# One norm scheme for both attention layers of a four-layer network, the last strip's convolution taps on GpSimd, and a new order of squares, means and index loads

## The chip, the cores and the metric

The kernel runs on one core of one Trainium2 chip. The metric is the device time of one execution in microseconds, the median of several runs. A core has five instruction queues that matter here: TensorE (PE), VectorE (DVE), ScalarE (ACT), GpSimd (POOL) and SyncE (SP). SP issues nearly all DMAs. Each queue runs its instructions in order.

## The reference

A batch of four images of 256 channels on 64 x 64 places goes through four layers, each `x = x + layer(gn(x))`. The change touches the two attention layers only:

```python
# gn: 32 groups of 8 channels; as written here a group's mean and variance are taken
# over axes 1, 2 and 4 of the view (B, H, W, G, C/G) of an array that holds (B, C, H, W)
x = x + _L0_conv_ref(_gn(x), ...)   # attention layer
x = x + _L1_conv_ref(_gn(x), ...)   # attention layer
x = x + _L2_conv_ref(_gn(x), ...)   # mamba layer
x = x + _L3_conv_ref(_gn(x), ...)   # grouped mamba layer

# an attention layer
y = mhsa(x, ...)                     # gated scan down the image (tanh, sigmoid, 1x1 convolutions)
qkv = to_windows(y) @ qkv_w.T + qkv_b            # 64 windows of 64 places
logit = einsum('bpc,bqc->bpq', q_win * SCALE, k_win)   # window means
_, idx = top_k(logit, 4)             # each window attends to the places of 4 windows
out = softmax(q k_g.T * SCALE) v_g   # 8 heads of 32
out = out + depthwise_conv3x3(v, lepe_w) + lepe_b
return out @ wo_w.T + wo_b
```

Since gn reads the array as (B, H, W, C), its groups are pairs of columns of the image: one mean and one variance for two columns over all channels and rows.

## The kernel before, in words

The four images are worked through one after the other, with x of one image held in SBUF (128 partitions x 2 x 4096). `attention_layers` runs two layers; each has a scan phase, `routing` and a window phase. An image is cut into eight strips of eight columns.

**Scan phase.** For each strip it takes the normalised x (`lay["xn"][s]`), makes two hidden layers and the gated scan into `y`, and one strip later the keys and values, which go to a DRAM buffer `kvd`, window by window. The values also go into `vimg`, over whose rows the 3 x 3 depthwise convolution is taken. The norm of the strips is laid in between by `gn_four`, two strips ahead; strips 0 and 1 must be there when the phase begins.

**Routing.** Window means give a 64 x 64 table of logits, and `idx` holds the places of the four best windows.

**Window phase** (`window_phase`, the object of the change). Its loop runs over 32 pairs of windows, i = 0 to 31, with `sj, a = divmod(i, 4)`: four pairs belong to strip sj. The order of all work is written out by hand. For pair i:

- `gather(i + 3)` issues eight DMAs of 128 KB from `kvd` into `kv` (eight buffers, so four pairs). `indices(i + 4)` loads the places into registers of SP before. For pairs 0 and 1 half of the gathers go through ACT's queue.
- `scores` (TensorE, L546) writes into two PSUM buffers, h = 0 and 1. `smallest` (DVE, L558) reduces them to the least value, since the scores are held with the opposite sign. `exps` (ACT, L569) takes exponentials and sums. `normalise` takes the reciprocal (DVE, L581) and scales eight slices on POOL (L584). `turn` (TensorE, L597) transposes, `turned` evicts half on DVE (L608) and half on ACT (L610). `values` (TensorE, L623) multiplies with the values, and `own_rows` (DVE, L634) adds the result to `vimg`.
- In pairs a = 1 and 2, `project` (TensorE, L233) multiplies the strip before with `wo` and its `add` (DVE, L644) adds the result to x. In four pairs a query of strip 6 or 7 is made. `double` moves queries to the other half of the partitions.

Beside this main work each pair carries extra steps from lists:

- `taps`: steps of the convolution of the last two strips on POOL, one a pair. A tap there is a weigh (L254, tile `tap`, tag "sq", one buffer) and an add (L257); the first one of a half is L269. There are 17 steps for each half m of the channels. `dve_taps` are nine single instructions on DVE (L271) for m = 0 of strip 7, popped in pairs with a = 0 or 3.
- `mids` and `ends`: steps of the norm. If a second attention layer follows (`nxt`), strips 0 and 1 of x are normalised by `gn`: sums (DVE, L143), a matmul for the mean (L134), the difference on POOL (L151), its square on ACT (L156, tag "sq"), a reduction on DVE (L160), a matmul, and the scaling on POOL (L168 a power of -0.5, L172). Otherwise `stats` takes only the statistics of strips 0 to 6, for the mamba layer: sums (L200), matmul (L195), mean (L206), four squares of x with the mean as bias, each with its sum (ACT, L215), matmul, variance (L221).
- Results of these small matmuls, projections and queries share one PSUM buffer, tag "mm".

At the start of the phase SP runs `indices(0)`, gathers 0 to 2 with their indices from `idx`, then `load_row`: two DMAs (L493, L494) that bring all places through DRAM into one row of a partition, from which pairs 4 and on are loaded. In the first layer `load_scan_weights(nxt)` (L115, 1 MB) follows.

Of the kernel before, what the change touches and what calls it, by code (L numbers as in the profile page):

```python
# [44 lines left out]
class Net:  # L45
# [33 lines left out]
    def attention_layers(self, x, w_drams, v_drams):  # L79
        tc, nc = self.tc, self.nc  # L80
        with ExitStack() as ctx:
# [107 lines left out]
            def stats(s, psum):  # L189
# [20 lines left out]
                def square(g):  # L210
                    if g == 0:
                        box["s2"] = self.small.tile([P, 4], F32, tag="gn_s2", name="gn_s2")
                        box["sq"] = norm.tile([P, 2, 8, S], F32, tag="xn", name="gn_sq")
                    two = slice(2 * g, 2 * g + 2)
# [5 lines left out]
                def variance():  # L220
                    nc.vector.tensor_copy(self.gvar[:, 4 * s : 4 * s + 4], box["pv"][:, 0:4])  # L221

                return (
                    sums, lambda: columns("pm", box["s1"]), mean,
                    *(lambda g=g: square(g) for g in range(4)),
                    lambda: columns("pv", box["s2"]), variance,
# [250 lines left out]
            def window_phase(lay, work, psum, idx, nxt, taps):  # L477
# [21 lines left out]
                def indices(i):  # L499
                    if 3 < i < n_pair:  # L500
# [150 lines left out]
                indices(0)  # L651
                for i in range(3):
                    gather(i)
                    indices(i + 1)
                load_row()
# [5 lines left out]
                taps = taps + lepe(lay, NW - 1, pool=True)[17:]  # L661
                dve_taps = lepe(lay, NW - 1)[:9]

                mids, ends, left = {}, {}, []
# [8 lines left out]
                if nxt:  # L673
                    load_scan_weights(nxt)
                    for s in range(2):
                        i = 7 + 4 * s
                        plan(gn(nxt, s, lambda: psum), (ends, i), (ends, i + 1), (mids, i + 2),
                             (ends, i + 3), (mids, i + 4), (ends, i + 4), (mids, i + 5))
                else:

                    for s in range(NW - 1):
                        i = 4 * s + 7
                        plan(stats(s, lambda: psum), (ends, i), (ends, i + 1), (mids, i + 2),
                             (ends, i + 2), (mids, i + 3), (ends, i + 3), (mids, i + 4),
                             (ends, i + 4), (mids, i + 5))
                for i in range(n_pair):
# [3 lines left out]
                    if i:  # L690
# [3 lines left out]
                        turn(i - 1, 1)  # L694
                        smallest(i, 1)
# [6 lines left out]
                    normalise(i, 0)  # L702
                    if a == 3 and sj + 2 in (NW - 2, NW - 1):
# [17 lines left out]
                    for t in taps[i : i + 1]:  # L721
                        t()
                    if a in (0, 3) and i and dve_taps:
                        dve_taps.pop(0)()
# [9 lines left out]
                    indices(i + 4)  # L734
# [1437 lines left out]
```

## Time and profile before

| | us |
|---|---|
| median of 3 runs | 11914.07 (11912.61 to 11917.38) |
| profiled execution | 11903.13 |
| its span | 11901.3 |
| first-layer window phases, first to last L584 | 254.8, 251.6, 248.0, 251.2 |
| second-layer window phases, first to last L584 | 224.5, 223.4, 231.3, 233.5 |

The span is the time from the first to the last instruction of the profiled execution. A row of the busy times by stage gives start and end in us, the length, then for each engine its busy time and the number of instructions, then the granted TensorE clock (1.00 is full speed), the share of the DMA engines and GB/s. In a timeline row stand start, duration, engine, line, operation, output and inputs, shapes, and in brackets how long the engine had been idle and what ended that. PEld is the loading of weights into TensorE. A queue letter behind an engine's name (SPq) marks what its sequencer does, such as issuing a DMA.

### The profile page before, as it was taken

How to read it: one execution, taken by the hardware profiler on the slowest of the kernel's cores; microseconds unless marked ns; L12 is line 12 of the kernel's file. 1: busy time of each engine (PE TensorE's matmuls, PEld its weight loads, DVE VectorE, ACT ScalarE, POOL GpSimd, SP SyncE). 2: the span in 40 equal slices, each digit the busy share in tenths (PEclk: the TensorE clock that was granted, in tenths of full speed). 3: DMA queues.
4: the chain of work that ended last, by engine and by line, in shares of the span. 5: the costliest groups of instructions: out<-in, count | busy, mean ns of one | idle time of the engine just before them, and what ended most of it. 6: DMA issues, size and time to landing. Idle time of an engine off the chain costs nothing. (4 is left out here: it accounts for less than half of the span.)

```text
span 11901.3 us, 192225 instructions
## 1 busy us (share of the span) xinstructions
PE 10069.9 (85%) x71104; PEld 5762.7 (48%) x71104; DVE 9868.8 (83%) x8422; ACT 7006.9 (59%) x13096; POOL 8695.6 (73%) x5918
## 2 busy tenths in 40 slices
PE   8998887777899888777789988877778998887777
PEld 4564454444456455444445645544444564554444
DVE  6677998998767799899866779989987677998998
ACT  4565554776456555577645655557764565555776
POOL 4566886898456688689845668868984566886897
PEclk9998998999999899899999989989999998998998
DMA  3344454554334455455433445545543344554554
GB/s 96 101 133 137 173 178 144 171 181 159 89 99 137 138 172 175 147 169 181 157 88 101 133 139 172 176 147 169 181 158 92 98 134 139 173 175 145 169 175 154
DMA packets 682505, 1742.09 MB, mean 146 GB/s; under 512 B 88896, under 2 KB 194896, under 8 KB 681312
## 3 DMA queue, kind: packets, MB, share of 16 engines
q1 hardware_dynamic: 676448, 1721.41, 44.7%
q8 instruction: 563, 9.22, 0.3%
q10 hardware_dynamic: 5120, 8.39, 0.3%
q14 instruction: 374, 3.06, 0.1%
HBM read 1601.52 MB, written 94.39 MB: 142 GB/s over the span
## 5 line engine op out<-in xcount | busy, mean ns | idle before, releaser
L1016 POOL TENSOR_TENSOR hc<-h,cb 128x1024 f32<-128x1024 f32 x2056 | 4807.7, 2350 | 785.6 <-DVE h L1010 341.4
L1010 DVE TENSOR_TENSOR_SCAN h<-da,m_state,pb 128x1024 f32<-128x1024 f32 x1248 | 2920.2, 2340 | 163.1 <-DVE pb L1004 4.3
L962 PE MATMUL y<-ident,hc 128*128 128x128 f32 x16384 | 2345.2, 290 | 404.4 <-POOL hc L1016 333.7
L962 PEld LDWEIGHTS y<-ident,hc 128*128 128x128 f32 x16384 | 2043.7, 150 | 1127.6 <-POOL hc L1016 575.0
L1004 DVE TENSOR_TENSOR pb<-du,pb 128x1024 f32<-128x1024 f32 x1672 | 2024.4, 1211 | 118.9 <-PE pb L934 116.8
L946 ACT ACTIVATE da<-delta,m_v 128x1024 f32<-128x1024 f32 x1672 | 1899.4, 1141 | 135.7 <-DVE h L1010 118.9
L934 PE MATMUL pb<-m_parts,pick 128*128 128x512 bf16 x3312 | 1081.8, 411 | 835.0 <-DVE h L1010 768.7
L584 POOL TENSOR_SCALAR pr<-pr,sm,zero 128x256 f32<-128x256 f32 x2048 | 1136.1, 569 | 533.6 <-DVE sm L581 530.2
L569 ACT ACTIVATE pr<-sc,mn 128x256 f32<-128x256 f32 x2048 | 952.7, 477 | 552.4 <-DVE sm L581 359.9
L934 PEld LDWEIGHTS <-pick 128*128 128x128 bf16 x3312 | 264.0, 101 | 1779.8 <-DVE h L1010 977.2
L558 DVE TENSOR_REDUCE mn<-sc 128x4 f32<-128x1024 f32 x512 | 629.6, 1231 | 528.3 <-PE sc L546 527.0
L1010 DVE TENSOR_TENSOR_SCAN h<-da,pb 128x1024 f32<-128x1024 f32 x424 | 969.3, 2286 | 55.6 <-ACT m_u L1704 0.5
L920 POOL TENSOR_TENSOR bb<-du,bb 128x1024 f32<-128x1024 f32 x376 | 888.5, 2363 | 118.7 <-DMA bb<-m_cd 108.3
L597 PE MATMUL pt_ps<-ident,pr 128*128 128x128 f32 x4096 | 663.9, 297 | 85.0 <-POOL pr L584 40.2
L1010 DVE TENSOR_TENSOR_SCAN h<-dap,m_state,bb 128x1024 f32<-128x1024 f32 x288 | 672.2, 2334 | 65.9 <-ACT dap L946 46.1
L233 PE MATMUL conv_ps<-att_y,att_wb 128*128 128x512 f32 x1536 | 686.7, 597 | 3.0 <-DVE gvar L221 3.0
L546 PE MATMUL sc<-kv,q_swap 32*64 32x128 f32 x8192 | 599.4, 286 | 11.4 <-DMA kv<-kv_dram 8.8
L946 ACT ACTIVATE dap<-delta,m_v 128x1024 f32<-128x1024 f32 x376 | 419.8, 1116 | 308.5 <-DVE h L1010 245.8
L546 PE MATMUL sc<-kv,att_y 32*64 32x128 f32 x7168 | 580.1, 287 | 17.4 <-DMA kv<-kv_dram 13.7
L597 PEld LDWEIGHTS pt_ps<-ident,pr 128*128 128x128 f32 x4096 | 471.5, 148 | 225.6 <-POOL pr L584 138.4
L271 DVE SCALAR_TENSOR_TENSOR lp<-vimg,att_v,lp 128x512 f32<-128x512 f32 x672 | 507.7, 755 | 30.8 <-DVE lp L271 1.0
L546 PEld LDWEIGHTS sc<-kv,att_y 32*64 32x64 f32 x7168 | 434.0, 139 | 153.3 <-issue 58.8
(300 smaller groups left out, 17799.4 us busy)
## 6 DMA issues: line engine op xcount, KB each, us to landing
cb<-m_cd SPq DMA_DIRECT2D x2048, 512.0 KB, 3.8
kv<-kv_dram SPq DMA_DIRECT2D x1984, 128.0 KB, 2.8
bb<-m_cd SPq DMA_DIRECT2D x376, 512.0 KB, 5.5
kv_dram<-kst SPq DMA_DIRECT2D x128, 256.0 KB, 3.9
kv_dram<-vn SPq DMA_DIRECT2D x128, 256.0 KB, 4.1
q_swap<-att_y SPq DMA_DIRECT2D x96, 256.0 KB, 4.4
m_pe<-in_pe_dram SPq DMA_DIRECT2D x32, 512.0 KB, 4.5
out_dram<-yo SPq DMA_DIRECT2D x64, 256.0 KB, 2.4
```

Source lines behind the costliest of these rows:

```text
L233: nc.tensor.matmul(ps, w[:, k, w0 + m * P : w0 + (m + 1) * P], src[:, k], start=(k == 0), stop=(k == 1),)
L546: nc.tensor.matmul(sc[h][b * 64 : b * 64 + 64, r, w, m, :], (own(sj, m) if r == b else swap[sj % 2][:, m])[rows, 2 * a + w], kv[i, w][rows ...
L569: nc.scalar.activation(t[:, g].rearrange("p j r t -> p r j t"), sc[h][:, :, g // 2, g % 2, :].rearrange("p r (j t) -> p r j t", j=2), AF.E ...
L584: nc.gpsimd.tensor_scalar(t[:, g], t[:, g], s[:, g : g + 1], self.zero, ALU.mult, ALU.add)
L597: nc.tensor.transpose(pt[h][j][:, g, :], t[:, g, j].rearrange("p r t -> p (r t)"), self.ident,)
L920: nc.gpsimd.tensor_tensor(pb[i], slots[i][0]["du"], pb[i], ALU.mult)
L934: nc.tensor.matmul(pb[i][:, ss], self.pick[:, n : n + 1].to_broadcast([P, P]), blk["parts"][:, ss], start=True, stop=True,)
L946: nc.scalar.activation(da[i], blk["delta"], AF.Exp, scale=blk["a"](n))
L962: nc.tensor.matmul(blk["y"][:, ss], t[:, ss], self.ident, is_transpose=True, start=(n == 0 and ss.start % NT == 0), stop=(n == DS - 1 and ...
L1004: nc.vector.tensor_tensor(pb[i], blk["du"], pb[i], ALU.mult)
L1010: nc.vector.tensor_tensor_scan(h[i][:, ss], da[i][:, ss], pb[i][:, ss], state, ALU.mult, ALU.add)
L1016: nc.gpsimd.tensor_tensor(hc[i][:, ss], h[i][:, ss], cb[i][:, ss], ALU.mult)
```

## The change

The diff in full. `gn` for the next layer is replaced by `stats` with two new steps: `deviation` (the power over 4 columns) and `scale` (per two columns, subtract the mean and multiply, from x, on POOL), at the ends of pairs 13, 14 (strip 0) and 17, 18 (strip 1). The tile of the squares becomes the normalised tile. Both layers now use one plan: the mean goes to a new list `begins`, run before `smallest(i, 1)`; the squares lie in pairs a = 1 and 2, two each; the variance or deviation is in `begins` too. All 34 steps of strip 7's taps are on POOL; a second step is popped in pairs a = 1, 2, between the two `normalise`. `load_row` comes ahead of the first gather, and pairs 2 and 3 take their places from the row as well. `load_scan_weights` is called in pair 4.

```diff
@@ stats
-            def stats(s, psum):
+            def stats(s, psum, lay=None):
...
                         box["sq"] = norm.tile([P, 2, 8, S], F32, tag="xn", name="gn_sq")
+                        if lay:
+                            lay["xn"][s] = box["sq"]
...
+                def deviation():
+                    rstd = self.small.tile([P, 8], F32, tag="gn_rstd", name="gn_rstd")
+                    box["rstd"] = rstd = rstd[:, 0:4]
+                    nc.vector.tensor_scalar(rstd, box["pv"][:, 0:4], 1e-5, None, ALU.add)
+                    nc.gpsimd.tensor_tensor(
+                        rstd, rstd, self.minus_half.to_broadcast([P, 4]), ALU.pow
+                    )
+
+                def scale(*gs):
+                    for g in gs:
+                        two = slice(2 * g, 2 * g + 2)
+                        nc.gpsimd.tensor_scalar(
+                            box["sq"][:, :, two], xs[:, :, two], box["mean"][:, g : g + 1],
+                            box["rstd"][:, g : g + 1], ALU.add, ALU.mult,
+                        )
+
                 return (
                     sums, lambda: columns("pm", box["s1"]), mean,
                     *(lambda g=g: square(g) for g in range(4)),
-                    lambda: columns("pv", box["s2"]), variance,
+                    lambda: columns("pv", box["s2"]),
+                    *((deviation, lambda: scale(0, 1), lambda: scale(2, 3)) if lay else (variance,)),
                 )
@@ window_phase
                 def indices(i):
-                    if 3 < i < n_pair:
+                    if 1 < i < n_pair:
...
                 indices(0)
+                load_row()
                 for i in range(3):
                     gather(i)
                     indices(i + 1)
-                load_row()
...
-                taps = taps + lepe(lay, NW - 1, pool=True)[17:]
-                dve_taps = lepe(lay, NW - 1)[:9]
-
-                mids, ends, left = {}, {}, []
+                last_taps = lepe(lay, NW - 1, pool=True)
+                taps = taps + last_taps[17:] + last_taps[:17]
+
+                begins, mids, ends, left = {}, {}, {}, []
...
-                if nxt:
-                    load_scan_weights(nxt)
-                    for s in range(2):
-                        i = 7 + 4 * s
-                        plan(gn(nxt, s, lambda: psum), (ends, i), (ends, i + 1), (mids, i + 2),
-                             (ends, i + 3), (mids, i + 4), (ends, i + 4), (mids, i + 5))
-                else:
-
-                    for s in range(NW - 1):
-                        i = 4 * s + 7
-                        plan(stats(s, lambda: psum), (ends, i), (ends, i + 1), (mids, i + 2),
-                             (ends, i + 2), (mids, i + 3), (ends, i + 3), (mids, i + 4),
-                             (ends, i + 4), (mids, i + 5))
+                for s in range(2 if nxt else NW - 1):
+                    i = 4 * s + 7
+                    plan(stats(s, lambda: psum, nxt), (ends, i), (ends, i + 1), (begins, i + 2),
+                         (mids, i + 2), (ends, i + 2), (mids, i + 3), (ends, i + 3),
+                         (ends, i + 4), (begins, i + 5), (ends, i + 6), (ends, i + 7))
...
                         turn(i - 1, 1)
+                        for t in begins.get(i, ()):
+                            t()
                         smallest(i, 1)
...
                     normalise(i, 0)
+                    if a in (1, 2) and taps:
+                        taps.pop(0)()
...
                         own_rows(i - 1)
-                    for t in taps[i : i + 1]:
-                        t()
-                    if a in (0, 3) and i and dve_taps:
-                        dve_taps.pop(0)()
+                    if taps:
+                        taps.pop(0)()
...
                     indices(i + 4)
+                    if i == 4 and nxt:
+                        load_scan_weights(nxt)
                     for t in ends.get(i, ()):
                         t()
```

## The prediction

> **What bounds the kernel now.** I read the page first, then cut the trace by stage. The page gives no engine as the bound:
>
> ```profile
> span 11901.3 us, 192225 instructions
> PE 10069.9 (85%) x71104; PEld 5762.7 (48%) x71104; DVE 9868.8 (83%) x8422; ACT 7006.9 (59%) x13096; POOL 8695.6 (73%) x5918
> ```
>
> The change lies in the window phases alone, two in each of the four batches. I marked each by the first and the last normalising instruction on POOL (L584): the first layer's four take 254.8, 251.6, 248.0 and 251.2 us, the second layer's 224.5, 223.4, 231.3 and 233.5. Both run the same 32 pairs; they differ in the norm work laid beside them. So I cut them at pairs 7 and 19, and summed the busy times of pairs 7 to 18, where the first layer prepares strips 0 and 1 of its successor. First layer (one row of four, then the sum over the four), then second layer:
>
> ```profile
> 290.77:399.52 108.75, 95.78 (x1754) 71.64 (x1747) 67.59 (x105) 60.15 (x219) 77.90 (x115) 0.80 0.46 134
> sum 437.52, PE 380.20 PEld 285.35 DVE 270.13 ACT 240.69 POOL 311.54; mean PE 95.05 PEld 71.34 DVE 67.53 ACT 60.17 POOL 77.89
> ```
>
> ```profile
> 753.81:838.38 84.57, 80.12 (x1756) 59.27 (x1749) 65.49 (x105) 66.90 (x241) 65.89 (x109) 1.00 0.60 167
> sum 346.82, PE 325.94 PEld 243.97 DVE 261.75 ACT 267.88 POOL 263.52; mean PE 81.48 PEld 60.99 DVE 65.44 ACT 66.97 POOL 65.88
> ```
>
> The reader is to see 437.52 against 346.82 us, no engine full in the slower, and a granted TensorE clock of 0.80 there against 1.00. The timeline of the first layer says why (POOL, ACT, DVE and POOL rows of one pair):
>
> ```profile
> 317.62 1.19 POOL L257 TENSOR_TENSOR vimg<-vimg,tap 128x512 f32<-128x512 f32 x1
> ...
> 318.85 1.06 ACT L156 ACTIVATE gn_sq<-att_xn 128x1024 f32<-128x1024 f32 x1 [4.89 <-POOL vimg L257]
> 319.93 1.22 DVE L160 TENSOR_REDUCE gn_s<-gn_sq 128x4 f32<-128x1024 f32 x1 [1.23 <-ACT gn_sq L156]
> ...
> 322.59 1.63 POOL L584 TENSOR_SCALAR pr<-pr,sm,zero 128x256 f32<-128x256 f32 x3 [3.78 <-DVE sm L581]
> ```
>
> The square sits in ACT's order ahead of the exponentials, and cannot start until the tap's add on POOL has freed the one "sq" buffer that both use. ACT stands 4.89 us, DVE stands behind the square with the reduction, and POOL then waits 3.78 us for the reciprocal queued behind that. All of it is one queue waiting for another.
>
> **The change, part by part.** "Per phase" is one window phase; there are four of each layer.
>
> *Norm of the next layer by the second layer's scheme (first layer).* Per strip it removes POOL 2.46 (L151) + 1.63 (L168, 8 columns) + 1.90 (L172), ACT 1.06 (L156), DVE 1.22 (L160). It adds four ACT squares with sums at 0.76 (L215), a power over 4 columns and four POOL scalings of 128x256. Squares read x and no shared buffer, so the wait above has no cause left; the second layer runs this scheme beside the same pairs in 346.82/4 = 86.7 us where the first takes 437.52/4 = 109.4. That is -22.7 per phase. POOL's additions are not in the second layer: the power costs between nothing and its 8-column row of 1.63 (it starts a pair in which POOL is nearly full), the scalings 0.57 each by the L584 row, 1.14 in each of two pairs. Of 2 x (1.63 + 2.28) = 7.8 us per phase I put 2.5 on the path, since the next normalising mostly waits for its reciprocal; ends 0 and 7.8.
>
> *Taps.* Nine DVE taps (mean 0.96, L271) go; POOL gets 17 more steps: first and eight weighs at 0.77, eight adds at 1.18, 16.4 us per phase. Fourteen of them fall between the two normalisings of pairs a = 1, 2, where POOL already stands idle:
>
> ```profile
> 766.81 2.16 POOL L584 TENSOR_SCALAR pr<-pr,sm,zero 128x256 f32<-128x256 f32 x4
> 771.18 2.17 POOL L584 TENSOR_SCALAR pr<-pr,sm,zero 128x256 f32<-128x256 f32 x4 [2.20 <-DVE sm L581]
> ...
> 778.39 2.16 POOL L584 TENSOR_SCALAR pr<-pr,sm,zero 128x256 f32<-128x256 f32 x4 [1.65 <-DVE sm L581]
> ```
>
> The smaller gap, 1.65, holds the longer step, 1.18. The other three come after pairs 25 to 27. I cost all at 0; if the gaps close, up to 16.4. The Trainium skill speaks against the move: its "GPSIMD Engine Reference", section 4.1 (Engine selection), sends elementwise adds to VectorE, GpSimd being about half as fast with two inputs. In engine time that holds here (0.77 + 1.18 against 0.96), and a sum by it would be 16.4 - 8.6 = +7.8 per phase, +62 in all. I go by the gaps, because DVE, not POOL, is last in pairs a = 3. The second layer, pairs 7, 11, 19, 23 and 27:
>
> ```profile
> 753.81:760.65 6.84, 6.13 (x160) 4.74 (x156) 6.11 (x10) 4.83 (x19) 5.89 (x9) 1.00 0.52 158
> 781.80:788.70 6.90, 6.18 (x166) 5.06 (x162) 6.17 (x11) 4.90 (x19) 5.51 (x9) 1.00 0.64 184
> ...
> 838.38:846.88 8.50, 7.67 (x151) 5.26 (x150) 6.08 (x11) 5.47 (x20) 5.50 (x9) 1.00 0.52 151
> 869.52:876.73 7.21, 7.01 (x151) 5.09 (x150) 5.20 (x10) 5.48 (x20) 5.08 (x9) 1.00 0.58 169
> 899.35:905.51 6.16, 5.65 (x154) 4.68 (x146) 5.38 (x10) 4.90 (x19) 4.33 (x8) 1.00 0.60 168
> ```
>
> Pairs 23 and 27 have the same sums of the norm and no DVE tap: 6.2 instead of 6.8 to 7.3 (pairs 7, 11, 15), 7.2 instead of 8.5 with a query (19). So -0.7, -0.7, -1.1, -1.3 = -3.8 per second-layer phase. In pairs a = 0 nothing: DVE idles 0.3 us there after the tap. What is late next is the supply of keys and values: SP issues eight gathers a pair, and waits for little:
>
> ```profile
> SPq L524 <- PE pt_ps L597: 8.4, 20, 1.5
> SPq L524 <- PE ov_ps L623: 2.9, 5, 1.4
> ```
>
> With four smaller rows SP waits 14.1 us of 210; it issues for 93% of the phase. Shorter pairs shorten the gathers' lead. I take back a third: -2.5. In the first layer only pairs 7, 11 and 15 gain: -1.5.
>
> *Squares with projections, means early.* The mean no longer waits behind the reduction of scores (L558), so it frees the "mm" buffer for the projection; TensorE's waits for it are 0.15 to 0.6 us. The squares move into ACT gaps of 0.9 and 1.3 us in pairs a = 1, 2. -1.0 per second-layer phase; ends 0 and -3.
>
> *Places and weights (queue of SP).* The two DMAs of load_row move ahead of the first gather, and the second waits for the first to land (1.66 us); the scan weights, 1 MB, leave the head of the phase for pair 4.
>
> ```profile
> 240.02 0.48 SPq L493 DMA_DIRECT2D listed<-idx  x1
> 241.69 0.82 SPq L494 DMA_DIRECT2D row<-listed  x1
> 242.57 0.40 SPq L115 DMA_DIRECT2D att_wa<-in_l_w_dram  x1
> ```
>
> ```profile
> 251.54 0.40 PE L546 MATMUL sc<-kv,att_y 32*64 32x128 f32 x2 [2.38 <-DMA kv<-kv_dram]
> ...
> 256.27 1.97 PE L597 MATMUL pt_ps<-ident,pr 128*128 128x128 f32 x8
> ```
>
> Ahead of the gathers SP holds 0.48 + 1.2 + 0.82 = 2.5 us more, but until the keys' writes have landed it waits anyway (222.8 to 224.4). The first gather moves from 224.6 to about 225.6. In the first layer the scores wait for it (0.57 us at 231.89): +1.0; in the second a query's eviction ends last: +0.5. Places of pairs 2 and 3 cost one load of 0.52 in place of two of 0.31: nothing.
>
> The weights at the head delay gather 3: pairs 0 to 6 take 203.18/4 = 50.8 us in the first layer, 189.91/4 = 47.5 in the second: -3.3. At pair 4 they stand behind gather 7 and a swap of 0.5 MB, and ahead of gather 8, needed some 10.7 us later; issuing takes 6 and landing 2.8, so about 2 us are to spare against a transfer of some 4.3 (1 MB at the busy share of a gathering pair, 0.59 x 7.2). What would a stall cost? After the 2.38 us wait, eight transposes take 1.97 instead of 1.09 until 268, and pairs 2 and 3 of that phase lose 8.1 us against the second layer's. The page "TensorE: Matmul & The Clock Gate", part 1, lets the clock return after some 3.4 us of busy TensorE; by that the stall would cost 2.4 + 1.7 = 4.1. The trace decides: 8.1 at worst, 3.3 on the mean. For the new place: between 0 and 8.1; I take 1.5, nearer to hidden.
>
> **Sum per batch.** First layer: -22.7 + 2.5 - 1.5 - 3.3 + 1.5 + 1.0 = -22.5. Second: -2.5 - 1.0 + 0.5 = -3.0. Four batches: -102. The profiled execution took 11903.1; the median shown is 10.9 above it. 11801 + 11 = 11812.
>
> **The rivals.**
> - *Gathers become the bound.* SP's 93% and waits of 2 to 3 us for keys in single pairs a = 3 speak for it; it takes the second layer's gain (3.5) and leaves the first layer 8 us short of its own: -14 per batch, 11858. Against: strips with full clock show 0.2 to 0.5 us of such waits.
> - *The stalls only change owner.* Power and scalings are POOL steps in the same pairs as before, with two taps each in pairs 13, 14, 17 and 18. At their upper end, 7.8, they cost 5.3 more per phase than I put, and a stall with a half clock behind it some 5: +10.3 per batch, 11853. Against: between those pairs' normalisings POOL has gaps.
> - *Slower: POOL's taps land on the path.* If the first normalising arrives late in a = 1, 2, each of the 17 steps delays the second one, and the transposes and values behind it: 16.4 x 8 = +131, so 11943. It decides from 102/131, 78% of the steps, on. Against: gaps of 1.65 and 2.20.
>
> **How the numbers follow.** Forecast case 0.72 (its own range 11780 to 11845), gathers 0.14, owner 0.08, taps 0.06. A measurement of this kernel tells 0.2%, 24 us, from no change; only the last case, and a sliver of the two before it, come below that. The range reaches up to the second and third cases, and down to all prices at their low end (-34 per batch, and a few us from a steadier clock).
>
> **What would show it.** No ACT wait for a tap; pairs 7 to 18 of the first layer near 88 us each phase, its phases near 229, TensorE's clock near 1.0 there; second-layer phases near 225; pairs 11, 15 and 19 shorter by about 1 us; the second normalising of pairs a = 1, 2 still waiting for the reciprocal. I am wrong if POOL's normalising starts straight after a tap and transposes wait for it, if scores of pairs 7 to 9 wait for keys behind the weights, or if the first layer stays above 240.

## The result and the profile after

| | median us | lowest to highest | runs |
|---|---|---|---|
| before | 11915.72 | 11912.61 to 11921.65 | 4 |
| changed | 11812.20 | 11795.75 to 11822.70 | 4 |

The ratio is 0.9911, with a 95% interval of [0.9894, 0.9928]: some 104 us less. The profiled execution of the changed kernel took 11811.95 us, 91.2 less than that of before (11903.1). The difference of the medians is larger because the profiled execution of before lay 10.9 us below the median that the prediction started from, and this one lies at its own. Note the spread, too: the changed kernel's four runs cover 27 us, so a term of less than some 10 us cannot be told by a median, and the points below that are smaller rest on the traces. A trace is one execution, and its waits wander too, as a second trace of the changed kernel shows below.

The head of the page after:

```profile
span 11810.1 us, 191909 instructions
PE 9965.7 (84%) x70632; PEld 5738.0 (49%) x71104; DVE 9804.7 (83%) x8342; ACT 7028.2 (60%) x13152; POOL 8773.6 (74%) x6070
```

No engine's share tells the gain. DVE lost 64 us of busy time and POOL gained 78, in the direction in which the taps went. So the same cuts as in the prediction: pairs 7 to 18, one row for each of the four batches and their sum. First layer:

```profile
285.33:375.88 90.55, 85.16 (x1764) 64.57 (x1764) 60.39 (x97) 65.79 (x238) 76.52 (x125) 0.92 0.59 165
3226.80:3313.62 86.82, 81.15 (x1763) 60.35 (x1762) 60.00 (x97) 65.80 (x238) 76.57 (x125) 0.98 0.61 167
6174.88:6270.60 95.72, 88.39 (x1764) 67.56 (x1764) 60.30 (x97) 65.91 (x238) 76.53 (x125) 0.88 0.58 165
9130.02:9215.42 85.40, 81.76 (x1765) 61.49 (x1764) 60.03 (x97) 65.38 (x237) 76.56 (x124) 0.97 0.57 162
sum 358.49, PE 336.46 PEld 253.97 DVE 240.72 ACT 262.88 POOL 306.18; mean PE 84.11 PEld 63.49 DVE 60.18 ACT 65.72 POOL 76.54
```

The sum was 437.52 and is 358.49. The granted clock of the four rows was 0.80, 0.74, 0.84 and 0.86, and is 0.92, 0.98, 0.88 and 0.97. Second layer, the sum alone (346.82 before):

```profile
sum 347.26, PE 325.09 PEld 247.70 DVE 242.42 ACT 269.12 POOL 274.61; mean PE 81.27 PEld 61.92 DVE 60.60 ACT 67.28 POOL 68.65
```

There DVE's busy time fell by 19 us and POOL's rose by 11, and the length did not move. By whole phases, summed over the four batches in microseconds:

| | before | after |
|---|---|---|
| first layer, pairs 0 to 6 | 203.2 | 187.9 |
| first layer, pairs 7 to 18 | 437.5 | 358.5 |
| first layer, pairs 19 on | 364.9 | 367.3 |
| second layer, pairs 0 to 6 | 189.9 | 186.8 |
| second layer, pairs 7 to 18 | 346.8 | 347.3 |
| second layer, pairs 19 on | 376.0 | 380.3 |

The first layer's phases gave 91.9 us, the second layer's took 1.7. The rest of the kernel takes 9983.0 us before and 9982.0 after in these two traces. POOL beside the first layer's pairs, where before the square of the norm stood behind the tap's add:

```profile
305.30 2.16 POOL L603 TENSOR_SCALAR pr<-pr,sm,zero 128x256 f32<-128x256 f32 x4 [1.06 <-DVE sm L600]
307.44 0.77 POOL L273 TENSOR_SCALAR tap<-vimg,att_v,zero 128x512 f32<-128x512 f32 x1
309.07 2.17 POOL L603 TENSOR_SCALAR pr<-pr,sm,zero 128x256 f32<-128x256 f32 x4 [0.86 <-DVE sm L600]
311.20 1.19 POOL L276 TENSOR_TENSOR vimg<-vimg,tap 128x512 f32<-128x512 f32 x1
```

and ACT in the same stretch:

```profile
307.50 0.80 ACT L217 ACTIVATE gn_sq<-x,gn_mean 128x256 f32<-128x256 f32 x1
```

The square now runs from 307.50 to 308.30, with a tap's weigh on POOL beside it and no wait. ACT's wait for a tap by the old square (eight times, 38.9 us in all before) is not in the waits of after. The second normalising still waits 0.86 us for DVE's reciprocal after a tap has been fitted in, so the tap lies in a gap there.

### The profile page after: what moved, and what is told of

It reads as the page before. It is cut to its first block, busy times and chain, and to the rows that moved or that the text cites. A ratio compares the mean times of both kernels' runs of the same rounds, so it can differ in the third digit from the quotient of the medians.

```text
span 11810.1 us, 191909 instructions
## 1 busy us (share of the span) xinstructions
PE 9965.7 (84%) x70632; PEld 5738.0 (49%) x71104; DVE 9804.7 (83%) x8342; ACT 7028.2 (60%) x13152; POOL 8773.6 (74%) x6070
## 5 line engine op out<-in xcount | busy, mean ns | idle before, releaser
L949 PE MATMUL pb<-m_parts,pick 128*128 128x512 bf16 x2840 | 976.1, 414 | 842.0 <-DVE h L1025 772.6
L603 POOL TENSOR_SCALAR pr<-pr,sm,zero 128x256 f32<-128x256 f32 x2048 | 1107.2, 556 | 385.5 <-DVE sm L600 381.0
L935 POOL TENSOR_TENSOR bb<-du,bb 128x1024 f32<-128x1024 f32 x376 | 888.3, 2363 | 118.1 <-DMA bb<-m_cd 110.1
L616 PE MATMUL pt_ps<-ident,pr 128*128 128x128 f32 x4096 | 637.9, 292 | 37.8 <-POOL pr L603 16.8
L616 PEld LDWEIGHTS pt_ps<-ident,pr 128*128 128x128 f32 x4096 | 459.3, 146 | 165.6 <-POOL pr L603 108.4
```

What stands on the lines that cost most here:

```text
L603: nc.gpsimd.tensor_scalar(t[:, g], t[:, g], s[:, g : g + 1], self.zero, ALU.mult, ALU.add)
L616: nc.tensor.transpose(pt[h][j][:, g, :], t[:, g, j].rearrange("p r t -> p (r t)"), self.ident,)
L935: nc.gpsimd.tensor_tensor(pb[i], slots[i][0]["du"], pb[i], ALU.mult)
L949: nc.tensor.matmul(pb[i][:, ss], self.pick[:, n : n + 1].to_broadcast([P, P]), blk["parts"][:, ss], start=True, stop=True,)
```

## The experiments

Each kernel is the changed one with the edit shown, except the first, which is the kernel before with one part. They were timed four or five times each, in three groups, each group on a chip of its own and beside the kernel before on that chip. That kernel's medians are 11913.42 us in the first group (norm_only to swap_act), 11914.89 in the second (swap_late to places_back) and 11905.06 in the third (the rest). The ratio given is to the kernel before of the same group. A difference from the changed kernel below is from its median of 11812.20, so between groups, and some 10 us of it mean nothing.

**The norm alone** (norm_only): the kernel before with the second layer's scheme of the norm in the first layer's phases, and nothing else. The lines that are left out give `stats` the two new steps, as in the change.

```diff
...
-                        plan(gn(nxt, s, lambda: psum), (ends, i), (ends, i + 1), (mids, i + 2),
-                             (ends, i + 3), (mids, i + 4), (ends, i + 4), (mids, i + 5))
+                        plan(stats(s, lambda: psum, nxt), (ends, i), (ends, i + 1), (mids, i + 2),
+                             (ends, i + 2), (mids, i + 3), (ends, i + 3), (mids, i + 4),
+                             (ends, i + 4), (mids, i + 5), (ends, i + 6), (ends, i + 7))
```

Expected: 

> The kernel before with one part of the change: the next layer's strips are normalised by the statistics scheme (four squares of x with sums, power over 4 columns, scalings from x), at the places where the second layer's statistics lay before. Taps, places, weights and the second layer stay. Theory: the first layer lost its time to the square that waited for the tap's buffer, so this part alone brings pairs 7 to 18 of the first layer from a sum of 437.5 us to 345 to 370, second layer unchanged within 6; in all -75 to -90 us. Rival: the stall only goes when the taps, the order of the squares or the weights move too; then the sum stays above 395 and the whole gains 45 us at most.

Measured: 11820.13 us (11815.15 to 11831.61), ratio 0.9919 [0.9905, 0.9932], so -93. First layer, pairs 7 to 18, one row and the sum:

```profile
290.51:377.30 86.79, 80.45 (x1763) 58.84 (x1759) 64.67 (x103) 65.31 (x238) 73.89 (x119) 1.00 0.60 170
sum 355.27, PE 327.59 PEld 241.59 DVE 258.50 ACT 261.55 POOL 295.64; mean PE 81.90 PEld 60.40 DVE 64.63 ACT 65.39 POOL 73.91
```

The sum is that of the changed kernel within 1%, with the nine DVE taps still in it (DVE 258.50 against 240.72). This part carries nearly the whole gain. By the medians all other parts together are worth 8 us, which the spread does not tell from nothing.

**The taps back on DVE** (taps_back):

```diff
-                last_taps = lepe(lay, NW - 1, pool=True)
-                taps = taps + last_taps[17:] + last_taps[:17]
+                taps = taps + lepe(lay, NW - 1, pool=True)[17:]
+                dve_taps = lepe(lay, NW - 1)[:9]
...
-                    if a in (1, 2) and taps:
-                        taps.pop(0)()
...
```

Expected: 

> The changed kernel with the taps as before: nine on DVE, one step a pair on POOL. Theory (supply of keys): DVE's taps in pairs a = 3 only lengthened pairs that now wait for keys instead, so this is within 12 us of the changed kernel, with fewer waits of scores for keys. Rival 1 (the prediction): the move was worth 2.5 us per second-layer phase and 1.5 per first, so this is 16 us slower. Rival 2: POOL's extra steps sit on the path, so this is 20 us or more faster.

Measured: 11808.79 us (11787.15 to 11816.58), ratio 0.9905 [0.9890, 0.9920]. In the total the move of the taps brought nothing. What the theory said of the waits came true: the scores' waits for keys, summed over TensorE and its weight loads, are 29.0 us here, against 47.9 with the taps moved (44.2 in the second trace of the changed kernel). The second layer's pairs 7, 11, 15 and 19, from which the taps were taken, add up to 121.0 us in the four batches here and to 129.6 in the changed kernel.

**The weights back at the head of the phase** (weights_head):

```diff
+                if nxt:
+                    load_scan_weights(nxt)
...
-                    if i == 4 and nxt:
-                        load_scan_weights(nxt)
```

Expected: 

> The changed kernel with the scan weights loaded at the head of the loop again. Theory: the stall moves and does not go: pairs 0 to 6 of the first layer get 10 to 15 us longer in the sum of four phases, pairs 7 to 18 some 10 to 16 shorter (pairs 7 and 8 no longer wait for gather 8): 0 to 5 us slower in all. Rival: the load at pair 4 is hidden and pair 7 waits for another reason (the swap before it); then pairs 7 to 18 stay at 358 and the whole is 12 us slower.

Measured: 11819.97 us (11814.29 to 11829.89), ratio 0.9921 [0.9908, 0.9935], 8 above the changed kernel and within the intervals. But the first layer's pairs 0 to 6 took 185.3 us, no more than the 187.9 with the weights at pair 4. So the weights at the head did not make those pairs long on their own. Pairs 7 to 18 stayed at 357.1 us, as the rival had it, and pair 7 fell only from 10.2 to 8.9. What made the head long before is seen in pair 2 of the first layer, whose length runs to the scores that need gather 3. The four batches of before, then with the row of places behind the three gathers but the weights in pair 4 (places_back, below), then with the weights at the head but the row ahead (this run):

```profile
sum 40.45, PE 33.05 PEld 26.95 DVE 17.08 ACT 19.64 POOL 20.29; mean PE 8.26 PEld 6.74 DVE 4.27 ACT 4.91 POOL 5.07
```

```profile
sum 29.70, PE 27.17 PEld 22.11 DVE 16.88 ACT 19.22 POOL 24.99; mean PE 6.79 PEld 5.53 DVE 4.22 ACT 4.80 POOL 6.25
```

```profile
sum 25.06, PE 22.62 PEld 17.71 DVE 17.11 ACT 19.61 POOL 24.88; mean PE 5.65 PEld 4.43 DVE 4.28 ACT 4.90 POOL 6.22
```

That is 10.1, 7.4 and 6.3 us a pair, and 6.2 in the changed kernel. It took the row and the weights together ahead of gather 3 to make the stall.

**The swaps issued by ACT** (swap_act). The swap of halves of a strip (two DMAs, or four for the last two strips) leaves SP's queue for ACT's:

```diff
-            def double(s):
+            def double(s, eng=nc.sync):
...
-                        nc.sync.dma_start(
+                        eng.dma_start(
...
-                        double(sj + 1)
+                        double(sj + 1, nc.scalar)
...
```

Expected: 

> The changed kernel with the swaps of queries in the window phase issued by ACT instead of SP; same bytes, same pairs. Theory: SP's issuing sets the pace of the gathers, and a swap puts it 1.4 to 2.6 us back once a strip, which is paid in pairs a = 3; off SP the waits of scores for keys fall to under half (47.9 us in all now), second-layer phases fall by 4 to 8 us each, the whole by 25 to 45 us. Rival: the transfers themselves (1 MB of keys and 0.5 MB of swap in a pair) are the limit; then the waits stay within a fifth and the time within 10 us, or grows by ACT's issuing, 0.6 us a DMA.

Measured: 11805.22 us (11794.06 to 11810.58), ratio 0.9903 [0.9888, 0.9918], 7 below the changed kernel. The total hardly moves, and the waits for keys, 38.6 us, did not fall to half as the theory had it. But the second layer's phases fall from 914.4 (909.1 in the second trace) to 891.0 us, 5.9 a phase. Why is seen in their pair 11, in the changed kernel first (four batches, then the sum):

```profile
752.68:762.07 9.39, 7.81 (x161) 6.69 (x157) 5.41 (x10) 4.95 (x19) 5.07 (x9) 0.82 0.60 162
3700.28:3711.09 10.81, 9.34 (x140) 8.02 (x134) 5.44 (x10) 4.95 (x19) 5.07 (x9) 0.56 0.57 165
6650.26:6656.35 6.09, 5.58 (x154) 4.73 (x147) 5.36 (x10) 4.83 (x19) 5.08 (x9) 1.00 0.53 148
9599.75:9609.16 9.41, 7.62 (x162) 6.50 (x157) 5.46 (x10) 4.95 (x19) 5.08 (x10) 0.82 0.58 166
sum 35.70, PE 30.35 PEld 25.95 DVE 21.67 ACT 19.68 POOL 20.30; mean PE 7.59 PEld 6.49 DVE 5.42 ACT 4.92 POOL 5.08
```

and the sum of the same pair with the swaps on ACT:

```profile
sum 24.95, PE 23.35 PEld 19.42 DVE 21.31 ACT 19.48 POOL 20.43; mean PE 5.84 PEld 4.86 DVE 5.33 ACT 4.87 POOL 5.11
```

The same instructions take 6.09 us at full clock in one batch and 9.4 to 10.8 in the three others, and 6.1 to 6.7 in all four with the swaps off SP. What the three have is a wait. SP's queue of the changed kernel, then TensorE, in the first batch:

```profile
743.83 1.35 SPq L328 DMA_DIRECT2D q_swap<-att_y  x2
747.07 12.34 SPq L543 DMA_DIRECT2D kv<-kv_dram  x16
```

```profile
748.76 1.09 PE L616 MATMUL pt_ps<-ident,pr 128*128 128x128 f32 x8
...
754.56 0.40 PE L565 MATMUL sc<-kv,att_y 32*64 32x128 f32 x2 [1.41 <-DMA kv<-kv_dram]
757.43 1.97 PE L616 MATMUL pt_ps<-ident,pr 128*128 128x128 f32 x8
```

A swap is issued at the end of pair 8; behind it stand the eight DMAs of gather 12, which the scores in pair 11 (they are those of pair 12) need. They wait 1.41 us, and the eight transposes after it take 1.97 us in place of 1.09 at full clock.

The swap is not the whole cause, since the batch without a wait (6650.26) has it in the same place. There gather 12 began 8.4 us before pair 11 (at 6641.84), and 5.6 to 5.9 us before it in the three others. That batch had waited before, in pair 7, which took 10.35 us there and 5.98, 8.23 and 7.98 in the others. The same holds in every second-layer phase of the changed kernel and of its variants with the swaps on SP whose pair 7 took 9.8 us or more: in all six, pair 11 took 6.1 or 6.2. While TensorE waits, SP's queue gets ahead, and the next swap is then covered. From the swap's start to the next gather's first DMA it is 3.1 to 3.8 us in all four.

The gain was not kept whole. The second layer's pairs 5, 9, 13 and 17, in front of which ACT now issues a swap, are 0.6 to 0.9 us longer each (pair 9 takes 32.49 us in the four batches against 28.92). A pair 8 and a pair 12 wait in this trace, in one batch each (9.1 and 10.2 us), and the first layer's phases came out at 921.3, against 913.7.

**The swaps on ACT and the weights in pair 29** (swap_late): the edit above, and

```diff
-                    if i == 4 and nxt:
+                    if i == 29 and nxt:
```

Expected: 

> The changed kernel with the window phase's swaps issued by ACT and the scan weights loaded in pair 29, after the last gather. Theory: pair 7 of the first layer (10.2 to 10.4 us on the mean with the weights in pair 4) waits for gather 8 behind the weights; with them gone it falls to 6 to 7, and the first layer's phases by 3 to 5 us each: 11785 to 11797. Rival: pair 7 waits because of the pace of issuing before it, whatever the weights do; then it stays above 9 and the time stays at 11805.

Measured: 11787.43 us (11773.01 to 11792.20), ratio 0.9889 [0.9874, 0.9904]. With its two variants below, this is the best version: its slowest run is below the changed kernel's fastest. The first layer's pair 7 (scores of pair 8, whose gather stands behind the weights) in the changed kernel, with only the swaps moved (swap_act), with only the weights moved (weights_late, below), and with both:

```profile
sum 40.94, PE 34.52 PEld 28.87 DVE 21.36 ACT 19.81 POOL 20.29; mean PE 8.63 PEld 7.22 DVE 5.34 ACT 4.95 POOL 5.07
```

```profile
sum 41.66, PE 35.95 PEld 29.73 DVE 21.35 ACT 19.79 POOL 20.41; mean PE 8.99 PEld 7.43 DVE 5.34 ACT 4.95 POOL 5.10
```

```profile
sum 32.95, PE 26.68 PEld 21.22 DVE 21.03 ACT 19.69 POOL 20.37; mean PE 6.67 PEld 5.30 DVE 5.26 ACT 4.92 POOL 5.09
```

```profile
sum 24.75, PE 22.84 PEld 17.88 DVE 20.64 ACT 19.37 POOL 20.43; mean PE 5.71 PEld 4.47 DVE 5.16 ACT 4.84 POOL 5.11
```

That is 10.2, 10.4, 8.2 and 6.2 us a pair. The weights alone make the whole stall, the swap alone half of it, so the two do not add up: only with both gone from in front of that gather does the pair run freely.

**More of SP's time** (sp_slow): from pair 7 on the kernel's text loads the places twice, which was to take some 15 us more of SP's time a phase.

```diff
+                        if 6 < i:
+                            loads, win = nc.values_load_multi_w_load_instructions(
+                                row[0:1, 2 * i : 2 * i + 2, :], engines=[ET.SP], min_val=0,
...
```

Expected: 

> The changed kernel with the places of each pair from 7 on loaded twice by SP: about 0.6 us more of SP's time in each of 25 pairs, 15 us a phase, and no byte moved more. Theory: SP's issuing paces the gathers, and its idle time of 11 to 19 us a phase lies mostly outside the strips that wait; then half or more of it shows: 6 to 12 us a phase, 50 to 100 us in all, waits of scores for keys at least doubled. Rival: the transfers limit, SP's waits swallow the loads: under 15 us in all.

Measured: 11829.45 us (11823.65 to 11835.76), ratio 0.9928 [0.9914, 0.9941], so +17. But the edit did not do what it was meant to do. The loads of places in the trace of the changed kernel, then in this one:

```profile
L520 SPq TENSOR_LOAD <-row x240: 520/526/2046, 231.7 to 9731.4; - x120
```

```profile
L526 SPq TENSOR_LOAD <-row x200: 520/526/1727, 267.5 to 9760.4; - x100
L520 SPq EVENT_SEMAPHORE  x200: 17/17/17, 267.4 to 9760.3; - x100
L520 SPq TENSOR_LOAD <-row x40: 520/525/542, 233.4 to 9576.4; - x40
```

There are 240 loads in both. In the program that ran, each doubled load is one load with a semaphore instruction of 17 ns ahead of it, so SP's added time is some 0.07 us apiece (from one start to the next), 14 us in the eight phases and not 120. The run therefore tests neither the theory nor its rival, and whether SP's issuing sets the pace of the gathers on the average stays open. The +17 and the waits for keys (58.7 us) belong to a kernel that differs from the changed one by those 14 us of SP's time at most.

**The order of means and squares as before** (order_back):

```diff
-                    plan(stats(s, lambda: psum, nxt), (ends, i), (ends, i + 1), (begins, i + 2),
-                         (mids, i + 2), (ends, i + 2), (mids, i + 3), (ends, i + 3),
-                         (ends, i + 4), (begins, i + 5), (ends, i + 6), (ends, i + 7))
+                    plan(stats(s, lambda: psum, nxt), (ends, i), (ends, i + 1), (mids, i + 2),
+                         (ends, i + 2), (mids, i + 3), (ends, i + 3), (mids, i + 4),
+                         (ends, i + 4), (mids, i + 5), (ends, i + 6), (ends, i + 7))
```

Expected: 

> The changed kernel with means, squares and variances at the places where the second layer had them before. Theory: the new order shortens pairs a = 1 and two pairs a = 0 of the second layer (3.2 us a phase by the pairs' lengths), and the next wait for keys takes it back; within 10 us of the changed kernel. Rival (the prediction): it is worth 1.0 us a phase net and upward, 4 to 13 us slower here.

Measured: 11815.97 us (11809.97 to 11817.48), ratio 0.9917 [0.9904, 0.9931]: 4 us off the changed kernel, that is none that can be told. The pairs show the order all the same. The second layer's pairs 20, 21, 24, 25 and 29 in the four batches, in the changed kernel and here:

```profile
sum 145.48, PE 143.57 PEld 103.03 DVE 97.24 ACT 125.00 POOL 107.71; mean PE 7.18 PEld 5.15 DVE 4.86 ACT 6.25 POOL 5.39
```

```profile
sum 154.45, PE 151.16 PEld 106.22 DVE 97.34 ACT 117.73 POOL 107.68; mean PE 7.56 PEld 5.31 DVE 4.87 ACT 5.89 POOL 5.38
```

With the order of before they are 9.0 us longer, 2.2 a phase (154.21 in the kernel before). The whole phases are not: 902.3 us here, 914.4 and 909.1 in the two traces of the changed kernel.

**The places as before** (places_back):

```diff
-                    if 1 < i < n_pair:
+                    if 3 < i < n_pair:
...
-                load_row()
                 for i in range(3):
                     gather(i)
                     indices(i + 1)
+                load_row()
```

Expected: 

> The changed kernel with the row of places loaded after the first three gathers again, and pairs 2 and 3 taking theirs from the table. Prediction: the row ahead of the gathers costs 1.0 us a first-layer and 0.5 us a second-layer phase at the start; 6 us faster here. Rival: the wait for the keys' writes covers it (the times from the places to the first normalising add up to 137.5 us against 136.3 before), within 5 us.

Measured: 11829.42 us (11810.04 to 11836.26), ratio 0.9927 [0.9914, 0.9941]. The prediction would have it 6 us faster, its rival within 5; it came out 17 slower, with intervals that meet. Loading the row ahead of the gathers does not cost 6 us and may bring some: with the row behind them, its two DMAs stand between the third gather and the fourth, and the first layer's pairs 0 to 6 took 192.1 us, against 187.9 and 185.3 in the two traces of the changed kernel. That is 4 to 7 of the 20 us by which the window phases of this trace are longer; the rest lies in later pairs. I call the sign shown only as far as "not a loss".

**The changed kernel once more** (after_again), in the third group.

Expected: 

> The changed kernel itself, on the chip of the next three runs, to compare them with it: 11805 to 11820. If a second profile puts the waits for keys into other pairs than the first did, single pairs of one trace can't be read as the price of an edit.

Measured: 11810.27 us (11793.99 to 11832.78), ratio 0.9918 [0.9904, 0.9931]. Its trace was of the longest run (span 11831.0), and its waits for keys lie in other pairs than in the first trace: pair 11 of the second layer takes 9.7 us there, pair 27 takes 6.4, against 8.9 and 9.9. A wait for keys in a single pair is not a property of the kernel; sums over four phases are steadier (1005.6 before, 913.7 and 915.8 in the two traces for the first layer). This execution is 21 us longer than the one traced first, and its window phases are 3 us shorter (1824.9 against 1828.1): the whole difference lies outside the part that the change touches.

**Do taps and order pay where the supply is loose?** (swap_late_taps, swap_late_order): the best version with the taps back on DVE, and with the order of before; the edits are those of taps_back and order_back on top of swap_late.

Expected of the first: 

> The version with swaps on ACT and weights in pair 29, with the taps as before (nine on DVE, one POOL step a pair). Theory: with the supply of keys loosened the move of the taps shows the worth that the prediction gave it, so this is 10 to 25 us slower than that version (11787), in pairs a = 3. Rival: the move is worth nothing whatever the supply does (DVE was last only by a few tenths); then within 8 us.

Expected of the second: 

> The same version with means, squares and variances at the places of before. Theory: with the supply loosened the order shows the 3 us a second-layer phase that its pairs' lengths promise: 8 to 16 us slower than 11787. Rival: ACT's issuing of the swaps now fills the gaps into which the squares went; then within 6 us, or faster.

Measured: 11789.95 (11774.48 to 11804.69) and 11788.89 us (11781.95 to 11791.51), ratios 0.9903 and 0.9901, beside 11787.43 and 0.9889. By the medians that is 2.5 and 1.5 us slower; with each set against the kernel before of its own group it is 12 and 11. The totals cannot decide between theory and rival. The pairs can, for the taps. The second layer's pairs 7, 11, 15 and 19 in the four batches, in the best version and with the taps back on DVE:

```profile
sum 103.90, PE 99.12 PEld 78.89 DVE 84.66 ACT 80.42 POOL 83.27; mean PE 6.20 PEld 4.93 DVE 5.29 ACT 5.03 POOL 5.20
```

```profile
sum 116.86, PE 109.06 PEld 83.22 DVE 98.14 ACT 80.33 POOL 89.64; mean PE 6.82 PEld 5.20 DVE 6.13 ACT 5.02 POOL 5.60
```

With the taps on POOL these pairs are 13.0 us shorter, 3.2 a phase, and the second layer's phases 13.9 (892.0 against 905.9). So where the supply is loose the move shows in the pairs in which it was forecast. The first layer's phases go the other way in these two traces, 904.1 with the taps on POOL and 893.8 with them on DVE, and the two cancel; 6.5 of these 10 us lie in pairs 0 to 6. With the order of before the picture is the same (892.5 in the first layer, 909.2 in the second). Each is one trace, and why the first layer is shorter is open.

**The weights in pair 29 alone** (weights_late), with the swaps on SP.

Expected: 

> The changed kernel with the scan weights in pair 29 and the swaps on SP as they were. Theory: pair 7 of the first layer falls from 10.2 to 8 us or less, and the whole by 10 to 18 us, the step from 11805 to 11787 that the same edit made with the swaps on ACT. Rival: with the swap in SP's queue pair 7 waits all the same; then within 6 us of the changed kernel.

Measured: 11808.64 us (11798.80 to 11817.17), ratio 0.9920 [0.9906, 0.9933]. Pair 7 falls to 8.2 us, as shown above, and the total stays (11810.27 for the changed kernel in the same group). The scores' waits for keys are 50.5 us in this trace, where the changed kernel has 47.9 and the best version 32.7: taken from one pair, they come back in others. Neither the swaps (-7) nor the weights (-4) alone can be told from nothing; the two together bring 25 in swap_late, and 22 and 23 in its two variants (20 and 21 against the changed kernel of their own group).

## Why the prediction was right, and where its steps were off

**The norm of the first layer (-22.7 per phase; -23.5 for all between the cuts, ahead of which the places lie): the size is right, and shown; the reason is shown in part.** The phase fell by 91.9/4 = 23.0 in the trace, and the norm alone brought 93 of the 104 us. Pairs 7 to 18 run at 89.6 us a phase (88 was named), at a clock of 0.88 to 0.98 (near 1.0 was named; the row of norm_only has it). The prediction's reason was the one buffer that the square shares with the taps. That loop is gone, but the new scheme also takes most of POOL's own work from in front of the normalising. TensorE and POOL before, around the stall that the prediction shows:

```profile
321.35 1.12 PE L597 MATMUL pt_ps<-ident,pr 128*128 128x128 f32 x4 [3.01 <-ACT pts L610]
...
330.81 1.64 POOL L168 TENSOR_TENSOR gn_rstd<-gn_rstd,minus_half 128x8 f32<-128x8 f32 x1 [1.61 <-DVE sm L581]
332.53 1.90 POOL L172 TENSOR_TENSOR att_xn<-att_xn,gn_rstd 128x1024 f32<-128x1024 f32 x1
334.42 4.74 POOL L584 TENSOR_SCALAR pr<-pr,sm,zero 128x256 f32<-128x256 f32 x8
```

The first row is the buffer's part: the transposes wait 3.0 us for an eviction that stands behind the square in ACT's queue, once a strip, 24.0 us in the eight strips, and norm_only has no such wait. The POOL rows are the other part: 3.5 us of power and scaling run straight into two normalisings. The transposes' waits for the normalising in pairs 7 to 18 fell from 20.8 to 8.2 us with norm_only. No run gave the square a buffer of its own, so how the gain divides between the two is not shown. It is shown what form it took: of the 82 us by which the sum fell in norm_only, 53 are TensorE's busy time for the same matmuls (380.20 before, 327.59 there), at a higher clock. By this estimate most of what the stalls cost was half clock, not waiting.

**Power and scalings on POOL (+2.5, bounds 0 and 7.8): the size held, its parts did not.** POOL at the end of such a strip:

```profile
325.28 1.01 POOL L229 TENSOR_TENSOR gn_rstd<-gn_rstd,minus_half 128x4 f32<-128x4 f32 x1
...
337.83 1.20 POOL L276 TENSOR_TENSOR vimg<-vimg,tap 128x512 f32<-128x512 f32 x1
339.00 1.54 POOL L236 TENSOR_SCALAR gn_sq<-x,gn_mean,gn_rstd 128x256 f32<-128x256 f32 x2
340.53 1.63 POOL L603 TENSOR_SCALAR pr<-pr,sm,zero 128x256 f32<-128x256 f32 x3
```

The power takes 1.01 us, between its bounds. A scaling takes 0.77, where 0.57 was taken from the normalising of the same shape. It reads a strip of x, whose rows do not lie one behind the other; that this is the reason is likely, but no run separates it. A tap, two scalings and the normalising follow each other without a gap, so here POOL's work is on the path. The pairs with scalings (13, 14, 17, 18) took 8.64, 7.71, 8.68 and 7.78 us in the mean, and 7.23, 7.20, 7.37 and 7.22 in the second layer: 3.8 per phase (2.5 in the second trace). The pairs 12 and 16 gave some 0.9 of it back in the first.

**Taps (-2.5 and -1.5 per phase): the step that failed.** They cost nothing, as predicted: TensorE's waits for POOL's normalising are no longer than with the taps on DVE (weight loads 108.4 us and matmuls 16.8, against 118.1 and 25.6 in taps_back), and the slower rival, in which each of the 17 steps delays the second normalising, found no place. But they brought nothing to the total either. What the prediction had wrong is the supply of keys, for which it took back a third of the 3.8 us a phase that it read from the pairs. All of it was taken back. The scores' waits for keys by TensorE and its weight loads, before and after:

```profile
PE sc L546 <- DMA kv<-kv_dram: 23.5, 41, 2.4
PEld sc L546 <- DMA kv<-kv_dram: 9.2, 16, 1.0
```

```profile
PE sc L565 <- DMA kv<-kv_dram: 32.9, 48, 3.1
PEld sc L565 <- DMA kv<-kv_dram: 15.0, 20, 1.9
```

They rose by 15 us, and without the moved taps they are at 29.0 again. Pairs 11, 15 and 19 of the second layer were to be some 1 us shorter each: 15 and 19 are, by 0.7 and 0.5 us in the mean, and 11 is 1.9 longer. Only in the batch where it did not wait is pair 11 shorter, 6.09 in place of 6.9. That is the rival "gathers become the bound", in the second layer only, where it was to take the 3.5 per phase that taps and order would bring; between the cuts the phase came out 0.4 longer, so 3.9 were lost. With the swaps on ACT and the weights late, pairs 7, 11, 15 and 19 are 3.2 us a phase shorter with the taps on POOL. So the 3.8 that was read from the lines was nearly right, and its discount was the term that was mis-sized. The sum by the rule on elementwise adds, +7.8 per phase, and the sum by gaps, -2.5, were both wrong for this kernel; by the traces it is +0.4 for taps, order and places together, 0 within the spread.

**Means and squares (-1.0): the pairs moved, the total did not.** The pairs that hold the squares and the means became shorter by 2.2 us a phase, in the changed kernel and in the best one alike (154.20 against 145.03 there). In the total that cannot be told from nothing, within the bounds 0 and -3.

**Weights (-3.3 at the head, +1.5 at pair 4): mis-sized.** Pair 7 was to show a wait of nearly nothing. It shows 10.2 us in the mean, 4.0 more than in the best version, where +1.5 was put. That scores of pair 7 wait for keys behind the weights was named as a sign of being wrong, and it came. The -3.3 was right as a sum (pairs 0 to 6 fell by 3.8 a phase) but put down to the weights alone: with the weights back at the head these pairs did not become longer, because the row of places had left as well. The total rose by 8 us, where the two terms would give 7, but the intervals of the two kernels overlap, so that this does not bear them out.

**Places (+1.0 and +0.5): the wrong sign, perhaps.** The way from the places to the first normalising grew by 1.2 us in the eight phases together (136.3 to 137.5), not by 6, and it is 137.5 with the row put back too. Putting it back did not gain time; in the first layer's pair 2 it lost 1.2 us a phase.

**The half clock.** The prediction weighed what a stall of 2.4 us would cost by "TensorE: Matmul & The Clock Gate", part 1 of the Trainium skill (4.1 us), which lets the clock return after some 3.4 us of busy TensorE, and by the trace (8.1 us). Pair 11 of the changed kernel shows both. The stretches at half clock that belong to the waits of the first batch (1.41 us) and of the second (1.47 us):

```profile
755.96:759.36 3.40, 3.40 (x74) 3.23 (x62) 3.00 (x5) 1.02 (x4) 2.11 (x4) 0.50 0.52 149
3701.66:3715.30 13.64, 13.24 (x227) 11.34 (x228) 6.76 (x11) 6.39 (x26) 6.25 (x12) 0.50 0.55 159
```

In the first the clock comes back after the page's 3.4 us; the price by it is 1.41 + 1.7 = 3.1, and that pair is 3.3 us longer than the one without a wait. In the second the clock stays at half for 13.6 us, though TensorE is busy for 13.24 of them and has no further wait once this one has ended at 3702.06; the pair is 4.7 us longer and the next one 1.8. So the page's rule gave the low end of what a stall costs here, and the upper end that the prediction took from the trace was needed. Why one stretch is four times as long as the other is open.

**The total** was forecast at 11812 and came out at 11812.2. That closeness is partly luck. Between the two profiled executions the sum is -91, not -102: the second layer's phases came out 14 us above their forecast (+1.7 in place of -12), with small amounts the other way. The profiled execution of before stood 10.9 below the median, that of after did not, and these 11 us filled the place.

**What stays open.** How the norm's gain divides between the shared buffer and POOL's own work. Why the two edits of the best version bring some 23 us together and not apart; the four lengths of pair 7 are part of the answer, since either transfer alone still stalls it. The waits wander between pairs in part because a wait in one strip gives SP's queue the lead that spares the next; what starts it in one execution and not in another is not settled. That the gather's place in SP's queue matters is shown for pair 11 and pair 7; whether SP's issuing or the transfers' own speed sets the pace of the whole is not tested.

## What to carry to other kernels

When no engine is full, look for side work that one queue lays in front of another's main work, and for a buffer that two engines' side work shares: an in-order queue that waits holds up everything behind. The norm's new scheme, which takes both away, was worth nine tenths of this change. Work moved off an engine is worth nothing to the total until the supply of the next stage is early enough; price it by doing it alone, and look at the pairs it was to shorten. Before a run that adds work is read, count in its trace that the work is there. In a queue that issues DMAs in order, place bulk transfers (swaps, weights) where no gather that is needed next stands behind them.

## What the runs showed of the hardware

- Short waits of TensorE cost more than their length here: a wait of 1.41 us made its pair 3.3 us longer, one of 1.47 us made its pair 4.7 and the next 1.8 us longer. The half clock behind them lasted 3.4 us in one case and 13.6 in the other.
- The pairs in front of which ACT issues a swap were longer: pair 9 of the second layer by 0.9 us ((32.49 - 28.92)/4), though ACT is busy only 6.3 of the 7.2 us there. The issuing of the two DMAs is the likely reason.
- A GpSimd scaling that reads strided rows took 0.77 us where the same shape with its rows in one piece took 0.54 (1.63 for three).
